# A graph layer on one core: 109 instead of 113 one-hot picked edge sets, 945 instead of 865 gathered chunks, and another order of the opening transfers

## The chip, the cores and the metric

The kernel runs on one core of one Trainium2 chip. The metric is the device time of one execution in microseconds, lower is better. A profile is one more execution under the hardware profiler; it has its own time and its own span, from the first to the last instruction. TensorE is called PE in the profile (PEld: its weight loads), VectorE DVE, ScalarE ACT, GpSimd POOL, SyncE SP; a letter q behind a name is that engine's instruction queue, which issues transfers and waits.

## The reference

There are 12,500 nodes with 128 features and 400,000 edges, sorted by destination, each of one of two types. Every edge carries its source's row through one of two weight matrices, and the messages are summed by destination:

```python
Xs = X[src]
m_data = Xs @ W_data.T + b_data
m_ctrl = Xs @ W_control.T + b_control
msg = jnp.where((edge_types == 0)[:, None], m_data, m_ctrl)
agg = jax.ops.segment_sum(msg, dst, num_segments=X.shape[0])
out = jax.nn.relu(agg + (X @ W_self.T + b_self))
return _layernorm(x + out, axis=-1)
```

## The kernel before

The kernel sums source rows first, by destination and type, and multiplies the sums by the weights afterwards. Each f32 row of x is split into three bf16 parts (high, middle, low) whose sum is the row; the parts stand in SBUF as `x3` and, written out, in DRAM as `rows3` (384 numbers per node).

**Two ways to fetch rows.** The 400,000 edges are 3125 chunks of 128, in 25 groups of 125 chunks. A group is laid out as five times 5 chunks for the first way and 20 for the second.

- *Gathered* chunks (`fetch`, L721; `gathered`, L727): GpSimd issues one indirect DMA that reads the 128 source rows of a chunk from `rows3` into `msg`. VectorE makes a one-hot matrix `psel` (edge by destination and type), once for a window of 5 or 25 chunks. TensorE then does four matmuls: the three parts of `msg` against `psel` (L671) and a column of ones against it, which counts edges (L747). They go to one PSUM bank `sums` for the whole window.
- *Picked* sets (`give_slots`, L518; `picked`, L753): a set is 20 chunks, 2560 edges. VectorE, with some matmuls of TensorE, gives each edge a place in a table of 100 cells by 32 places. The table goes to DRAM (`there`, L624) and comes back to all partitions (`pick`, L626), and VectorE turns it into one-hot columns (L656). TensorE picks the rows out of `x3` with them (`got`, L769), ScalarE casts them to bf16 (`emsg`, L780), and TensorE sums them by destination against a one-hot matrix `esel` (L671, counts in L798). Edges that find their cell full, at most 64, have their rows fetched by an indirect DMA of GpSimd (`last`, L784), the set's *spare rows*. The set's matmuls end with `last`.

In a group with fewer than five picked sets the last gathered window takes the remaining 20 chunks over: it has PL = 25 chunks instead of PB = 5. Before the change every odd group has four sets, every even one five (L175, L181): 113 sets, and 25 x 25 + 12 x 20 = 865 gathered chunks.

**Sums.** When a window or a set is finished, VectorE adds its PSUM bank into the accumulator `acc` of the group (`accumulate`, L702; the line in the profile is L709). A set's add has 352 elements per partition, a window's 160 or 480. There are two PSUM banks `sums` for sets and windows together. When the last window of a group is closed, the group is finished: `pass_on` (L695), then `finish`, which multiplies the sums by the weights (L894), applies the norm and writes out.

**Order.** The program is written as one loop over the sets (L981). Set w carries its own picking and summing, the slot work of sets w+2 and w+3, and its share of the gathered chunks, which are spread evenly over all sets from w = LAG = 2 on (L973). Message gathers are issued AHEAD = 14 chunks before use into HOLD = 18 buffers. A scheduler then orders each engine's instructions, so what stands next to each other in the code need not in the queue. Every engine works its queue in order; SP's transfers wait in order too.

**Opening.** The work from L947 on prepares group 0, splits x, makes the slots of sets 0 and 1, loads the edges of group 1 (`load(1, "e")`, `load(1, "p")`) and writes the bias rows: `bparts` (L395) splits the three biases into bf16 parts on one partition, then copies them into the rows of `bias` with 27 small DMAs (L405, L407). `bias` is first read by the first `finish`. After these come `store_rows` (L259), which writes `x3` to `rows3` in eight DMAs (L261), the first `prep_p`, and the first 14 gathers. All these transfers but x's own loads and the gathers are issued by SP. A gather, of messages as of spare rows, reads `rows3`, so it can run only when all eight stores have landed. The spare rows of a set are fetched at its step t = 2 of six (`spare_rows`, L782).

Of the kernel before, what the change touches and what calls it, by code (L numbers as in the profile page):

```python
# [9 lines left out]
BF = mybir.dt.bfloat16  # L10
# [7 lines left out]
P = 128  # L18
D = 128
# [4 lines left out]
NG = NC // GC  # L24
GN = P * GC * N // E
PB = 5
PL = 25
EC = 20
CQ = EC // 4
NE = 5  # L30
NWIN = 2 * NE
# [11 lines left out]
NQ = 25  # L43
NCELL = 4 * NQ
OVF = 64
# [106 lines left out]
def short_path(ctx, tc, const, ident, eps, wT, brow, bad, x, src, dst, etype, ws, bs, out):  # L152
    nc = tc.nc
    keep = ctx.enter_context(tc.tile_pool(name="keep", bufs=1))
    dram = ctx.enter_context(tc.tile_pool(name="dram", bufs=1, space=DRAM))
# [4 lines left out]
    two = ctx.enter_context(tc.tile_pool(name="two", bufs=2))  # L160
# [4 lines left out]
    def windows(g):  # L165

        c = g * GC
        for i in range(NE):
            yield "p", i, c, PB
            yield "e", i, c + PB, EC  # L170
            c += PB + EC

    def of_p(g, i):

        return PL if g % 2 and i == NE - 1 else PB  # L175

    def edges(a, c, n):
        return a[c * P:(c + n) * P].rearrange("(p c) -> p c", c=n)

    rows_p = (NE - 1) * PB + PL  # L180
    each_e = [(g, i) for g in range(NG) for i in range(NE - g % 2)]  # L181
    raw = {}
    starts = {k: [c for kind, _, c, _ in windows(0) if kind == k] for k in "pe"}
    gap = PB + EC
# [1 line left out]
    def load(g, kind):  # L186
        names = ("src", "dst", "typ")
        if kind == "e":
            raw[kind, g] = [ld.tile([P, NE, EC], I32, name=f"e{name}") for name in names]
            c = g * GC + starts["e"][0]  # L190
            for t, a in zip(raw[kind, g], (src, dst, etype)):
                at = a[c * P:(c + gap * (NE - 1)) * P].rearrange("(i k) -> i k", k=gap * P)[:, :EC * P]
                nc.sync.dma_start(out=t[:, :NE - 1, :], in_=at.rearrange("i (p c) -> p i c", c=EC))
                nc.sync.dma_start(out=t[:, NE - 1, :], in_=edges(a, c + gap * (NE - 1), EC))
        else:
            raw[kind, g] = [ld.tile([rows_p, P], I32, name=f"p{name}") for name in names]
            c = g * GC
            for t, a in zip(raw[kind, g], (src, dst, etype)):
                for i in range(NE):
                    b, n = c + starts["p"][i], PL if i == NE - 1 else PB  # L200
                    nc.sync.dma_start(
                        out=t[i * PB:i * PB + n, :], in_=a[b * P:(b + n) * P].rearrange("(c p) -> c p", p=P)
                    )
# [18 lines left out]
    for kind, i, c, _ in windows(0):  # L222
        if kind == "p":
            n = PL if i == NE - 1 else PB
            nc.sync.dma_start(
                out=near_i[i * PB:i * PB + n, :],
                in_=dst.rearrange("(o g e) -> o g e", o=1, g=NG)[:, :, c * P].to_broadcast([n, NG]),
# [6 lines left out]
    rows3 = dram.tile([N, 3 * D], BF, name="rows3")  # L234
# [44 lines left out]
    bias = keep.tile([P, 2, D], BF, name="bias")  # L279
# [77 lines left out]
    def places_and_weights():  # L357
# [34 lines left out]
            nc.tensor.transpose(wps[:, i * D:(i + 1) * D], wn[:, i, :], ident)  # L392
        nc.scalar.copy(wT, wps[:, :3 * D].rearrange("p (i d) -> p i d", d=D))

    def bparts():  # L395

        part = tmp.tile([1, 3, 3, D], BF, name="part")
        rest = tmp.tile([1, 3, D], FP, name="rest")
        nc.vector.tensor_copy(part[:, 0], brow)
        nc.vector.tensor_tensor(rest, brow, part[:, 0], op=OP.subtract)  # L400
        nc.vector.tensor_copy(part[:, 1], rest)
        nc.vector.tensor_tensor(part[:, 2], rest, part[:, 1], op=OP.subtract)
        for at in [at + k for at in range(0, P, CAP) for k in (0, 3)]:
            for j in range(3):
                nc.sync.dma_start(out=bias[at + j:at + j + 1, :, :], in_=part[:, j, 0:2, :])  # L405
        for j in range(3):
            nc.sync.dma_start(out=bias[6 + j:7 + j, 0, :], in_=part[:, j, 2, :])  # L407


    codes = {}  # L410
# [19 lines left out]
    def prep_p(g):  # L430

        s, d, t = raw.pop(("p", g))
        n = rows_p
        sf = pre.tile([n, P], FP, name="psf")
        rel = pre.tile([n, P], FP, name="prel")

        def first():
            nc.vector.tensor_copy(sf, s)
            nc.vector.tensor_scalar(rel, d, raw["near"][:, g:g + 1], None, op0=OP.subtract)
            codes["n", g] = code_of(rel, t, PW, 0, "p")  # L440

        def then():
            ps = ps1.tile([P, 512], FP, name="fin")
            nc.tensor.transpose(ps[:, :n], sf, ident[:n, :n])
            nc.tensor.transpose(ps[:, 128:128 + n], codes.pop(("n", g)), ident[:n, :n])
            idx = pre.tile([P, n], I32, name="pidx", bufs=3)
            nc.scalar.copy(idx, ps[:, :n])
            codes["p", g] = (idx, twice("pcol2", ps[:, 128:128 + n]))

        return [first, then]  # L450
# [19 lines left out]
    slots = {}  # L470
# [190 lines left out]
    acc, added, parts_in = {}, [], {}  # L661
# [32 lines left out]

    def pass_on(g):  # L695

        assert parts_in[g] == NWIN - g % 2
        if g + 1 < NG:
            begin_acc(g + 1)
            added.append(nc.vector.tensor_add(acc[g + 1][:, :, :lap], acc[g + 1][:, :, :lap], acc[g][:, :, GN:]))  # L700
# [26 lines left out]
    def gathered(g, i):  # L727
# [22 lines left out]

        return evenly([lambda c=c: chunk(c) for c in range(n)])

    def picked(w, tiled, ending, fin_used, before):  # L753

        g, i = each_e[w]
        s = {"sel": {}, "msg": {}}
        per, pair = 4, 2

        def choose(q0, n=8):

            sel = select(sp.tile([P, 9, 2 * EW], BF, name="esel")[:, :n], code_col, slots[w]["code"][:, q0:q0 + n])
            for k in range(n):
                s["sel"][q0 + k] = sel[:, k]

        def pick(ps, q, a0=0):
            for a in range(a0, 4):
                nc.tensor.matmul(  # L769
                    ps[CAP * a:CAP * (a + 1), :], slots[w]["pick"][:, a * NQ + q, :],  # L770
                    x3[:, 4 * q + a - a0].rearrange("p j d -> p (j d)"), start=True, stop=True, skip_group_check=True,
                )

        def rows(q):
            ps = psg.tile([P, pair, 512], FP, name="got")
            msg = two.tile([P, pair, 3 * D], BF, name="emsg", bufs=5)
            for k in range(pair):
                pick(ps[:, k, :3 * D], q + k)
                s["msg"][q + k] = msg[:, k, :]
            nc.scalar.copy(msg, ps[:, :, :3 * D])  # L780

        def spare_rows():  # L782
            msg = s["msg"][NQ - 1] = two.tile([P, 3 * D], BF, name="last")
            nc.gpsimd.indirect_dma_start(  # L784
                out=msg[:OVF, :], out_offset=None, in_=rows3[:, :],
                in_offset=bass.IndirectOffsetOnAxis(ap=slots[w]["idx"], axis=0),
            )

        def last_rows():
            q = NQ - 1  # L790
            ps = psg.tile([P, pair, 512], FP, name="got")[:, 0] if fin_used else ps1.tile([P, 512], FP, name="fin")
            pick(ps[:, :3 * D], q, 2)
            nc.scalar.copy(s["msg"][q][OVF:, :], ps[OVF:, :3 * D])

        def count(q):
            if q == 0:
                s["ps"] = sums()
            nc.tensor.matmul(  # L798
                cells_of(s["ps"], EW, 1)[CAP * (q % 4):CAP * (q % 4 + 1), :], one_col[:, :CAP], s["sel"][q],
                start=(q < 4), stop=(q + 4 >= NQ), skip_group_check=True,  # L800
            )

        def add(q0, q1):
            for q in range(q0, q1):
                add_rows(cells_of(s["ps"], EW, 0), s["msg"].pop(q), s["sel"][q], False, q == NQ - 1)

        def unit(t):

            for q in range(t * per, (t + 1) * per, pair):
                rows(q)  # L810
            if t == 1 and before:
                before()
            if t in (0, 1):
                choose(8 * t)
            if t == 0:
                ending()
            if t == 2:
                spare_rows()
            if t == 3:
                choose(16, 9)  # L820
            if t > 0:
                for q in range((t - 1) * per, t * per if t < turns - 1 else NQ):
                    count(q)
            if t == turns - 1:
                last_rows()
            if t > 0:
                add((t - 1) * per, t * per)
            for u in tiled.get(t, []):
                u()

        def end():

            add((turns - 1) * per, NQ)
            for u in tiled.get(turns, []):
                u()
            accumulate(g, 2 * i + 1, s["ps"], EW, EW)

        turns = (NQ - 1) // per
        return evenly([lambda t=t: unit(t) for t in range(turns)]), end


# [105 lines left out]
    split_units.pop(0)()  # L947
    prep_e(0)
    merged([(0.97, places_and_weights)], evenly(all_slots(0) + all_slots(1)), evenly(split_units))
    load(1, "e")  # L950
    load(1, "p")
    bparts()
    early.close()
    pro.close()
# [4 lines left out]
    for u in begin_slots(2):  # L959
        u()  # L960
    store_rows()
    for u in prep_p(0):
        u()
    for _ in range(AHEAD):
# [6 lines left out]
    for p in range(NG * NE):  # L971
        for _, u in gathered(*divmod(p, NE)):
            at = LAG + (n + 0.5) * (pairs - LAG) / total  # L973
# [206 lines left out]
```

## Time and profile before

| | us |
|---|---|
| median of 3 runs | 2086.24 |
| lowest and highest | 2075.97, 2093.50 |
| the profiled execution | 2095.26 |
| its span, first to last instruction | 2093.6 |

The profile's page has the busy time of each engine and its share of the span, the chain of work that ended last, and groups of instructions by line. A group's row reads: line, engine, operation, what it writes and reads, how often; then its busy time (the union of its instructions, in us), the mean duration of one in ns, and the idle time of the engine just before them with what ended most of it. A matmul's end is modelled and consecutive matmuls overlap, so the mean is longer than what one adds to a dense stream. A timeline's row reads: start, duration, engine, line, operation, what it writes and reads; in brackets the idle time before it and what ended it. Rows of the DMA queues give when a transfer was issued, not when it landed. The table of stretches gives, for each stretch, its length, the busy time of each engine with the number of its instructions, the granted clock of TensorE, the busy share of the DMA engines and their rate. TensorE's mean granted clock over the execution is 0.978. By the page's chain, 57% of the span is TensorE's, 28% VectorE's, 5% ScalarE's.

### The profile page before, as it was taken

To read this page: it belongs to the slowest core of one execution; us is meant where nothing else is said; L and a number is where in the kernel's file an instruction comes from. 1 tells how busy PE (TensorE), PEld (TensorE's weight loads), DVE (VectorE), ACT (ScalarE), POOL (GpSimd) and SP (SyncE) were. 2 spreads that over 40 slices of the span, in tenths; PEclk is the share of its full clock that TensorE was granted. 3 is DMA by queue.
4 is the path that set the end of the run, shared out by engine and by line. 5 is a ranking of instruction groups with operands and counts; after the bars stand their busy time and mean duration, and the time that the engine had idled before them with its cause. 6 is when DMAs were issued, how large, how long until landed. Compare 5 with 4: busy or idle time off the path is not lost.

```text
span 2093.6 us, 75473 instructions
## 1 busy us (share of the span) xinstructions
PE 1836.4 (88%) x30869; PEld 1376.5 (66%) x30869; DVE 1720.3 (82%) x4707; ACT 1304.5 (62%) x2464; POOL 1305.9 (62%) x996
## 2 busy tenths in 40 slices
PE   0669889999999998999999999999999999999996
PEld 0446667666766676666666666766776676766675
DVE  7958889888888888888888878878888888878873
ACT  4535666666666665666666666656666666656665
POOL 0167667667667566667666556575667667766760
PEclk9989999999999999999999999999999999999998
DMA  7643443443443443433433434434434434434321
GB/s 187 193 123 115 122 136 101 137 135 100 133 135 99 135 133 95 137 111 117 135 108 108 127 99 136 131 100 134 132 102 132 131 111 131 120 105 130 124 96 32
DMA packets 187343, 254.92 MB, mean 122 GB/s; under 512 B 86202, under 2 KB 153804, under 8 KB 183916
## 3 DMA queue, kind: packets, MB, share of 16 engines
q1 hardware_dynamic: 129226, 152.97, 22.7%
q0 software_dynamic: 45136, 90.65, 15.5%
q10 hardware_dynamic: 12626, 6.40, 1.2%
q8 instruction: 243, 3.98, 0.8%
q14 instruction: 112, 0.92, 0.1%
HBM read 231.87 MB, written 18.03 MB: 119 GB/s over the span
## 4 chain that ended last, share of the span: by engine, by line
PE 57%; DVE 28%; issue 5%; ACT 5%; DMA 2%; SPq 1%; POOL 1%; DVEq 0%; another core or an unknown queue 0%; ACTq 0%; POOLq 0%
PE sums L671 25%; PE got L769 19%; ACT emsg L780 4%; DVE esel L476 3%; PE rk L614 3%; DVE pick L656 3%; DVE prod L564 3%; DVE rv L602 2%; PE sums L798 2%; PE fin L894 2%; DVE found L573 2%; DVE prod L542 2%; PE rk L502 2%; DVE ahead L560 2%; PE rk L550 1%
## 5 line engine op out<-in xcount | busy, mean ns | idle before, releaser
L721 POOL DMA_INDIRECT msg<-rows,pidx x865 | 1167.3, 1350 | 697.9 <-PE sums L671 236.2
L780 ACT CAST emsg<-got 128x768 bf16<-128x768 f32 x1356 | 1036.1, 803 | 522.6 <-PE got L769 387.6
L671 PE MATMUL sums<-esel,emsg 128*128 128x176 bf16 x8136 | 761.9, 242 | 14.3 <-issue 13.4
L769 PE MATMUL got<-x,pick 128*32 128x384 bf16 x10896 | 663.5, 334 | 77.5 <-ACT emsg L780 43.8
L671 PEld LDWEIGHTS <-emsg 128*128 128x128 bf16 x8136 | 603.0, 99 | 174.6 <-issue 157.6
L769 PEld LDWEIGHTS <-pick 128*32 128x32 bf16 x11074 | 258.7, 95 | 232.6 <-issue 131.2
L476 DVE TENSOR_TENSOR esel<-code_col,code 128x1408 bf16<-128x1408 bf16 x339 | 308.6, 910 | 31.7 <-PE sums L671 14.1
L709 DVE TENSOR_TENSOR acc<-acc,sums 128x352 f32 (+2 forms) x238 | 102.0, 428 | 175.3 <-PE sums L671 85.8
L671 PE MATMUL sums<-psel,msg 128*128 128x48 bf16 x2595 | 187.3, 185 | 17.5 <-issue 7.2
L798 PE MATMUL sums<-esel,one_col 128*32 128x176 bf16 x2825 | 181.7, 244 | 7.0 <-issue 6.3
L784 POOL DMA_INDIRECT last<-rows,idx x113 | 134.4, 1189 | 56.4 <-issue 16.5
L671 PEld LDWEIGHTS <-msg 128*128 128x128 bf16 x2595 | 150.7, 98 | 26.0 <-issue 23.6
L614 PE MATMUL rk<-rv,O 128*128 128x64 bf16 x2260 | 90.8, 195 | 70.9 <-DVE rv L602 64.8
L656 DVE TENSOR_SCALAR pick<-pick,lane_f 128x1600 bf16<-128x1600 bf16 x226 | 143.2, 639 | 8.5 <-issue 5.0
L614 PEld LDWEIGHTS <-O 128*128 128x128 bf16 x2260 | 83.1, 100 | 99.2 <-issue 98.3
L747 PE MATMUL sums<-psel,one_col 128*128 128x48 bf16 x865 | 145.9, 183 | 0.5 <-issue 0.5
L476 DVE TENSOR_TENSOR O<-cell_col,blk 128x2000 bf16<-128x2000 bf16 x113 | 134.6, 1191 | 12.2 <-PE fin L769 4.7
L564 DVE TENSOR_TENSOR prod<-O,ahead 128x2000 bf16<-128x2000 bf16 x113 | 134.4, 1189 | 0.0
L560 DVE TENSOR_REDUCE ahead<-rk 128x100 bf16<-128x500 f32 x113 | 76.2, 674 | 53.5 <-PE got L769 21.0
L798 PEld LDWEIGHTS <-one_col 128*32 128x32 bf16 x2825 | 86.6, 96 | 47.5 <-issue 17.7
L747 PEld LDWEIGHTS <-one_col 128*128 128x128 bf16 x865 | 82.9, 96 | 1.0 <-issue 0.9
L573 DVE TENSOR_REDUCE found<-half 128x20 f32<-128x520 bf16 x113 | 77.1, 683 | 0.0
(173 smaller groups left out, 2030.2 us busy)
## 6 DMA issues: line engine op xcount, KB each, us to landing
pick<-there SPq DMA_DIRECT2D x113, 800.0 KB
acc<-acc_start SPq DMA_DIRECT2D x23, 1280.0 KB
msg<-rows,pidx POOLq DMA_INDIRECT x865
rows<-x SPq DMA_DIRECT2D x6, 1344.0 KB
xs<-in_x_dram SPq DMA_DIRECT2D x99, 62.5 KB
out_dram<-h SPq DMA_DIRECT2D x99, 62.5 KB
xt<-in_x_dram ACTq DMA_DIRECT2D x6, 896.0 KB
there<-cell SPq DMA_DIRECT2D x113, 6.2 KB
```

Of the source, the lines that this page charges most:

```text
L476: nc.vector.tensor_tensor(sel.rearrange("p n (w t) -> p n w t", t=2), col[:rows].rearrange("p (o w t) -> p o w t", o=1, t=2).to_broadcast( ...
L564: nc.vector.tensor_tensor(prod, s["O"], ahead.rearrange("p (o j) -> p o j", o=1).to_broadcast([P, EC, NCELL]), op=OP.mult)
L573: nc.vector.tensor_reduce(found, half[:, :, :26], AX.X, OP.add)
L614: nc.tensor.matmul(s["rk"][:m, :2 * CAP], s["held"][:, c * NCELL:c * NCELL + m], s["rv"][:, c].rearrange("p v r -> p (v r)"), start=(c == ...
L656: nc.vector.tensor_scalar(t, t, lane_f, None, op0=OP.is_equal)
L671: nc.tensor.matmul(out, msg[:, j * D:(j + 1) * D], sel, start=(start and j == 0), stop=stop, skip_group_check=True)
L721: nc.gpsimd.indirect_dma_start(out=msg[:, k, :], out_offset=None, in_=rows3[:, :], in_offset=bass.IndirectOffsetOnAxis(ap=codes["p", g][0] ...
L747: nc.tensor.matmul(cnt, one_col, sel, start=False, stop=(c == n - 1), skip_group_check=True)
L769: nc.tensor.matmul(ps[CAP * a:CAP * (a + 1), :], slots[w]["pick"][:, a * NQ + q, :], x3[:, 4 * q + a - a0].rearrange("p j d -> p (j d)"), ...
L780: nc.scalar.copy(msg, ps[:, :, :3 * D])
L784: nc.gpsimd.indirect_dma_start(out=msg[:OVF, :], out_offset=None, in_=rows3[:, :], in_offset=bass.IndirectOffsetOnAxis(ap=slots[w]["idx"], ...
L798: nc.tensor.matmul(cells_of(s["ps"], EW, 1)[CAP * (q % 4):CAP * (q % 4 + 1), :], one_col[:, :CAP], s["sel"][q], start=(q < 4), stop=(q + 4 ...
```

## The change

It has two parts. First, of three groups one now has five picked sets and two have four: groups 0, 3, 6, ..., 24 have five. In the others the last gathered window has 25 chunks. Second, the opening transfers are arranged anew: the biases' parts go to DRAM in one DMA (`b_parts`) and come back with nine (three rows at a time) in place of the 27 copies; the loads of group 1 are written behind the stores of `rows3`; the spare rows of set 0 are fetched ahead of the first 14 message gathers instead of in the middle of set 0.

```diff
+    def sets(g):
+        return NE if g % 3 == 0 else NE - 1
+
     def of_p(g, i):
-        return PL if g % 2 and i == NE - 1 else PB
+        return PL if sets(g) < NE and i == NE - 1 else PB
...
-    each_e = [(g, i) for g in range(NG) for i in range(NE - g % 2)]
+    each_e = [(g, i) for g in range(NG) for i in range(sets(g))]
...
+    b_parts = dram.tile([3, 3, D], BF, name="b_parts")
+
     def bparts():
...
         nc.vector.tensor_tensor(part[:, 2], rest, part[:, 1], op=OP.subtract)
+        nc.sync.dma_start(
+            out=b_parts.rearrange("j i d -> (j i d)").rearrange("(o e) -> o e", o=1),
+            in_=part.rearrange("o j i d -> o (j i d)"),
+        )
+
+    def bias_rows():
         for at in [at + k for at in range(0, P, CAP) for k in (0, 3)]:
-            for j in range(3):
-                nc.sync.dma_start(out=bias[at + j:at + j + 1, :, :], in_=part[:, j, 0:2, :])
-        for j in range(3):
-            nc.sync.dma_start(out=bias[6 + j:7 + j, 0, :], in_=part[:, j, 2, :])
+            nc.sync.dma_start(out=bias[at:at + 3, :, :], in_=b_parts[:, 0:2, :])
+        nc.sync.dma_start(out=bias[6:9, 0, :], in_=b_parts[:, 2, :])
...
-        assert parts_in[g] == NWIN - g % 2
+        assert parts_in[g] == NE + sets(g)
...
+    def spare_rows(w):
+        msg = slots[w]["last"] = two.tile([P, 3 * D], BF, name="last")
+        nc.gpsimd.indirect_dma_start(
+            out=msg[:OVF, :], out_offset=None, in_=rows3[:, :],
+            in_offset=bass.IndirectOffsetOnAxis(ap=slots[w]["idx"], axis=0),
+        )
...
             if t == 2:
-                spare_rows()
+                if w > 0:
+                    spare_rows(w)
+                s["msg"][NQ - 1] = slots[w]["last"]
...
     merged([(0.97, places_and_weights)], evenly(all_slots(0) + all_slots(1)), evenly(split_units))
-    load(1, "e")
-    load(1, "p")
     bparts()
...
     store_rows()
+    spare_rows(0)
+    bias_rows()
+    load(1, "e")
+    load(1, "p")
     for u in prep_p(0):
```

More of the change, by code (lines that the diff above doesn't have):

```diff
@@ L780, in rows @@
             nc.scalar.copy(msg, ps[:, :, :3 * D])
[L782 to L787, printed above, removed]
         def last_rows():
```

## Prediction

> **What bounds the kernel now.** I read the page's busy shares first, then busy time by stretch, then the timelines of the stretch that a stretch-table made look odd, then waits and groups for prices.
>
> ```profile
> span 2093.6 us, 75473 instructions
> PE 1836.4 (88%) x30869; PEld 1376.5 (66%) x30869; DVE 1720.3 (82%) x4707; ACT 1304.5 (62%) x2464; POOL 1305.9 (62%) x996
> ```
> ```profile
> core 0: us, PE busy (x) PEld busy (x) DVE busy (x) ACT busy (x) POOL busy (x), PEclk, DMA share, GB/s
> 60.00:95.14 35.14, 27.17 (x375) 17.34 (x375) 32.63 (x92) 21.93 (x44) 0.01 (x1) 1.00 0.56 170
> 95.14:126.20 31.06, 12.37 (x166) 8.41 (x168) 11.00 (x35) 8.16 (x17) 22.27 (x21) 0.71 0.54 169
> 126.20:2045.30 1919.10, 1760.38 (x29794) 1322.77 (x29787) 1614.62 (x4415) 1225.57 (x2336) 1277.47 (x956) 0.99 0.39 120
> ```
> Third row of the table: TensorE is busy for 92% of the long middle, VectorE 84%, GpSimd 67%, DMA 39%. The middle is TensorE's. Second row: from 95 to 126 us TensorE works 12.4 of 31.1 us. That is a hole in the opening.
>
> The middle is cut into sets by VectorE's add of a picked set into `acc` (128x352), once per set:
>
> ```profile
> 126.22 0.52 DVE L709 TENSOR_TENSOR acc<-acc,sums 128x352 f32 x1
> ...
> 2045.25 0.52 DVE L709 TENSOR_TENSOR acc<-acc,sums 128x352 f32 x1 [0.57 <-PE sums L671]
> ```
> These are sets 1 and 110 (counting from 0), so one set takes (2045.25 - 126.22) / 109 = 17.61 us. From the times of all such adds, the 24 sets in which a group is finished (L894) run 2.7 us longer than the rest; that part belongs to groups, not to sets.
>
> The hole, in the timelines of SP's queue, GpSimd and TensorE:
>
> ```profile
> 62.13 7.42 SPq L405 DMA_DIRECT2D bias<-part  x9
> ...
> 74.00 6.82 SPq L405 DMA_DIRECT2D bias<-part  x11
> 80.86 1.85 SPq L407 DMA_DIRECT2D bias<-part  x3
> 82.76 6.44 SPq L261 DMA_DIRECT2D rows<-x  x3
> ```
> ```profile
> 95.14 2.95 POOL L721 DMA_INDIRECT msg<-rows,pidx  x1 [90.33 <-DMA edst<-in_dst_dram]
> ...
> 115.72 0.91 POOL L784 DMA_INDIRECT last<-rows,idx  x1 [0.30 <-issue]
> 116.93 0.91 POOL L784 DMA_INDIRECT last<-rows,idx  x1 [0.30 <-issue]
> ```
> ```profile
> 118.34 0.62 PE L671 MATMUL sums<-esel,last 128*128 128x176 bf16 x3 [10.40 <-DMA last<-rows,idx]
> ```
> 27 small bias copies stand on SP in front of the last three pieces of `rows3`. No gather can run before these land, so GpSimd starts at 95.14. Fourteen message gathers then stand in front of the spare rows (`last`) of sets 0 and 1, and TensorE, done with the rest of both sets at 107.95, waits until 118.34.
>
> **The change: four sets fewer, 80 chunks more.** Groups 0, 3, ..., 24 (9) have five sets, 16 have four: 45 + 64 = 109 sets. Chunks: 25 x 25 + 16 x 20 = 945. They are spread over all sets but the first two, as now: 865 / 111 = 7.79 per set become 945 / 107 = 8.83. What a chunk costs TensorE is the open term:
>
> ```profile
> 1007.70 0.23 PE L671 MATMUL sums<-psel,msg 128*128 128x48 bf16 x3
> 1007.78 0.18 PE L747 MATMUL sums<-psel,one_col 128*128 128x48 bf16 x1
> 1007.89 0.51 PE L769 MATMUL got<-x,pick 128*32 128x384 bf16 x8
> ```
> ```profile
> L671 PE MATMUL sums<-psel,msg 128*128 128x48 bf16 x2595 | 187.3, 185 | 17.5 <-issue 7.2 <-DVE acc L709 7.2 <-DMA msg<-rows,pidx 1.4
> L747 PE MATMUL sums<-psel,one_col 128*128 128x48 bf16 x865 | 145.9, 183 | 0.5 <-issue 0.5
> ```
> From below: in a dense stretch (timeline) a chunk's four matmuls start at 1007.70 and the next work at 1007.89: 0.19 us. From above: the groups' busy time, (187.3 + 145.9) / 865 = 0.385 us, which counts the pipeline's drain where the next matmul already runs. I take 0.25, nearer to the direct reading. Then of a set's 17.61 us, 7.79 x 0.25 = 1.95 are chunks, 24 x 2.7 / 109 = 0.59 groups, and 15.07 the set itself. After: 15.07 + 8.83 x 0.25 + 24 x 2.7 / 105 = 17.89 us for each of the 105 sets between the same two marks: 1878.5 against 1919.0, a gain of 40. With 0.19 it is 46 (set alone 15.54, new period 17.83), with 0.385 it is 25 (14.02 and 18.04).
>
> A sentence beside it: the Trainium skill ("Perfetto Trace Analysis", Identifying the Most-Contended Engine) calls matmul busy time a bad measure, since matmuls are pipelined, and counts LDWEIGHTS busy instead. This profile's weight loads of a chunk, 150.7 + 82.9 us over 865, give 0.27 us and a gain of 38 by that rule; the trace agrees in so far as 0.27 lies between the two readings above.
>
> Off TensorE: VectorE loses four sets' work (1614.62 us over 109 sets, groups' work included: at most 14.8 us each) and gains 80 / 5 = 16 five-chunk selections' worth of work at 0.326 us: no new bound. ScalarE loses 48 copies of 0.80 us. GpSimd is the one engine that gains work:
>
> ```profile
> L721 POOL DMA_INDIRECT msg<-rows,pidx x865 | 1167.3, 1350 | 697.9 <-PE sums L671 236.2 <-PE got L769 178.5 <-DMA edst<-in_dst_dram 90.3
> ```
> A gather takes 1.35 us and 0.30 to the next: 1.65. With 1.5 for the set's `last` (1.19 + 0.30), a set takes 7.79 x 1.65 + 1.5 = 14.4 of 17.61 us now and 16.1 of 17.89 after, 90%. It now waits for TensorE to free buffers (236.2 and 178.5 us), and TensorE waited 1.4 us in all for a gathered message. So I cost it at nothing; the cover is some 1.8 us per set.
>
> **The change: the opening.** 27 bias copies (18.5 us of SP) become one write of `b_parts` and nine reads. In the built order of the changed program the stores of `rows3` stand among the loads of group 1, and the last one right behind set 1's `there` copy and `b_parts`; VectorE's order up to there is unchanged. Its last piece of x is done at 65.75, that `there` is ready at 68.2, so the store goes at about 69.5 instead of the three stores' 82.76 to 89.20. From the end of that issue to the first gather were 5.9 us: the gathers start at about 75.5, 20 us sooner. Set 0's `last` is first and lands by 78 (from its issue to landing 2.2 us). Behind it stand 18 gathers, 14 ahead and four of set 2, at 1.255 us (start to start here): set 1's `last` is issued at 75.5 + 1.25 + 22.6 = 99.3 and lands by 102, before TensorE needs it at 107.95. The 10.4 us wait is gone, and with it the slow train behind (add of set 0 at 124.04, 4.0 us more of TensorE idle for its bank). Set 1's add comes at about 108 instead of 126.2: a gain of 18. What is late next is TensorE's own stream of two sets. Bounds: up to 25 if the gaps of 0.4 us between its matmuls from 102 to 108 go too; 0 if another transfer takes the place.
>
> The wait that it adds: the bias reads wait on SP for `b_parts` to land. Queued behind: nine reads (0.6 us each by the rows above), the loads of group 1's edge types, group 2's edges and then set 2's `there`, which now goes at 89.30. `b_parts` goes at about 69; the worst small copy of this stretch, `there` at 53.48, landed after 7.3 us behind stores. 69 + 7.3 + 5.4 + 11 issues at 0.3 to 0.5 = 87: in time by 2 us, and each us beyond costs set 2 one. ScalarE's zeroing of `acc`, which shares memory with `part`, stands earlier in its queue and also waits for that copy, with set 0's casts behind: 0 to 3 us, inside the bounds.
>
> **Rivals.** (a) The opening gives nothing, since another transfer (the earlier stores compete with the fetches of x) delays the first `pick`. For it: DMA is 56% busy there. Against: the new order takes 17 issues off the queue. Gain 40 alone: 2086 - 40 = 2046.
> (b) The middle gives nothing: idle of TensorE (159 us of the 1919, 1.46 per set) grows because ScalarE's casts and the picks' matmuls alternate with more chunk matmuls between. It needs 0.39 us more per set, 41 in all. For it: 43.8 us of `got` waiting for casts. Gain 18 alone: 2068.
> (c) Slower: GpSimd already sets the pace. Its chunk then costs what it takes all in, (17.61 - 1.5) / 7.79 = 2.07 us, so a set takes 8.83 x 2.07 + 1.5 = 19.8 us, and 105 of them 2079: +160 - 18, or 2228. The change loses from 18.45 us per set on (1919 + 18 over 105), that is 1.92 us per gather. For it: by the trace, the 707 gathers and spare-row fetches beside which VectorE was busy for at least nine tenths of their first 0.9 us averaged 1.45 us, against 0.94 for the 85 beside which it was idle. Against: even 1.45 for all would be 8.83 x 1.75 + 1.5 = 17.0 us per set, and GpSimd waits for TensorE, not the reverse. The Trainium skill ("SBUF — State Buffer", A bandwidth-pool intuition that's wrong) says that a GpSimd-issued DMA of 620 ns takes about 3100 ns beside a VectorE copy, since VectorE locks out the writing of descriptors. At that length on every gather a set would be 8.83 x 3.4 + 1.5 = 31.5 us and the run over 3400, with no chance beside rows that stand at 17.61 with 7.79 chunks: the trace (mean 1.35, longest 4.26) bears out the lock, not that length.
> That the counts are not as said is no rival: the built order has 109 and 945.
>
> **How the numbers follow.** Likeliest: 40 + 18 = 58 less. The profiled execution took 2095.26 us (span 2093.6), 9.0 over the median of 2086.24; 2095.3 - 58 = 2037 on its own scale, 2028 on the median's. Its own range is 46 + 25 to 25 + 0 less: 2015 to 2061. Chances: forecast 0.68, (a) 0.17, (b) 0.09, (c) 0.06. A measurement here can tell about 1%, 21 us: faster below 2065 (forecast and (a), 0.85), within it (b), slower (c). For 8 in 10 the range takes in the forecast's ends, (a), and some 4 us of the runs' scatter: 2010 to 2064.
>
> **What would show it.** In the changed profile: the first gather near 75 and no wait for `last` near 10 us; set 1's add near 108; 105 periods of 17.9 us; GpSimd idle still ended by TensorE; TensorE's wait for messages still a few us. Wrong if the period exceeds 18.2, if GpSimd's idle is ended by nothing but issue, or if set 0 starts later than 69.

## The result, and the profile after

The changed kernel took 2190.87 us (median of 4 runs, 2187.47 to 2196.01), the kernel before beside it 2082.16 us (4 runs, 2075.97 to 2093.50): 1.049 times as long, 95% interval 1.0456 to 1.0525 (the two medians alone give 1.052; ratios here are always the recorded ones, differences in us are those of medians). Forecast were 2028 us and faster. The profiled execution took 2196.01 us with a span of 2193.9.

Page and table of stretches of the changed kernel, columns as before:

```profile
span 2193.9 us, 74107 instructions
...
PE 1859.7 (85%) x30253; PEld 1373.7 (63%) x30253; DVE 1673.0 (76%) x4583; ACT 1264.0 (58%) x2392; POOL 1397.7 (64%) x1072
```
```profile
core 0: us, PE busy (x) PEld busy (x) DVE busy (x) ACT busy (x) POOL busy (x), PEclk, DMA share, GB/s
60.00:77.10 17.10, 8.77 (x96) 5.24 (x96) 17.10 (x44) 7.60 (x15) 0.00 (x0) 1.00 0.77 268
77.10:107.80 30.70, 15.62 (x207) 9.86 (x206) 10.20 (x31) 11.99 (x22) 21.83 (x19) 0.78 0.43 127
122.71:2145.05 2022.34, 1780.63 (x29159) 1316.66 (x29156) 1566.94 (x4286) 1184.48 (x2263) 1366.21 (x1031) 0.96 0.38 116
```
In the long middle TensorE's share fell from 92% to 88%, VectorE's from 84% to 77%, ScalarE's from 64% to 59%. GpSimd's rose only from 67% to 68%. There is more time, and no engine fills it.

The sets' adds (timeline of VectorE; sets 0, 1 and 106):

```profile
107.25 0.52 DVE L719 TENSOR_TENSOR acc<-acc,sums 128x352 f32 x1 [20.08 <-issue]
...
122.19 0.52 DVE L719 TENSOR_TENSOR acc<-acc,sums 128x352 f32 x1 [0.38 <-PE sums L681]
...
2144.53 0.52 DVE L719 TENSOR_TENSOR acc<-acc,sums 128x352 f32 x1 [1.60 <-PE sums L681]
```
One set takes (2144.53 - 122.19) / 105 = 19.26 us, where 17.89 was forecast and 17.61 stood before. Over 105 sets the miss is 144 us, nearly all of the distance between forecast and result (163). Of the 1.65 us that a set takes longer than before, TensorE's busy rows hold 0.81 (16.15 to 16.96) and its idle time 0.84 (1.46 to 2.30).

TensorE's granted clock fell too, from 0.99 to 0.96 in the middle. By the clock's records it stood at half for 57 us of the middle before and for 143 us after. In these stretches TensorE began 9.9 and 8.1 instructions per us, in the rest 15.7 and 14.9. If the clock alone made that difference, it cost 21 us before and 65 after, so at most some 44 of the 173 us by which 105 periods grew. That is an estimate from these figures; what lowered the clock is not shown.

GpSimd's group on the page, its timeline in the opening, then TensorE's and ScalarE's in the same stretch:

```profile
L731 POOL DMA_INDIRECT msg<-rows,pidx x945 | 1260.6, 1334 | 636.4 <-PE sums L681 209.1
```
```profile
77.11 2.60 POOL L765 DMA_INDIRECT last<-rows,idx  x1 [72.30 <-DVE prod L574]
80.02 0.98 POOL L731 DMA_INDIRECT msg<-rows,pidx  x1 [0.30 <-issue]
...
103.47 0.95 POOL L731 DMA_INDIRECT msg<-rows,pidx  x1 [0.30 <-issue]
108.37 2.38 POOL L765 DMA_INDIRECT last<-rows,idx  x1 [3.95 <-DVE worst L426]
```
```profile
97.41 0.82 PE L786 MATMUL got<-x,pick 128*32 128x384 bf16 x6 [2.11 <-issue]
98.62 0.48 PE L786 MATMUL got<-x,pick 128*32 128x384 bf16 x1 [0.39 <-issue]
100.05 0.48 PE L786 MATMUL got<-x,pick 128*32 128x384 bf16 x1 [0.95 <-issue]
106.60 1.04 PE L786 MATMUL got<-x,pick 128*32 128x384 bf16 x8 [6.06 <-issue]
```
```profile
96.56 0.80 ACT L797 CAST emsg<-got 128x768 bf16<-128x768 f32 x1 [1.99 <-PE rk L512]
105.75 0.80 ACT L797 CAST emsg<-got 128x768 bf16<-128x768 f32 x1 [8.39 <-remote]
```
The gathers do start 18 us sooner (77.11 for 95.14). But while GpSimd issues them without a pause, TensorE does 16 matmuls in 10 us. The cast at 105.75 reads the eight matmuls whose last one ended at 100.05 + 0.48 = 100.53: it starts 5.2 us after its input was done by the profile, and the record of TensorE's completion signal, which ScalarE waits for, stands at 105.67. The eight matmuls at 106.60 then start 0.05 us after this cast's end (105.75 + 0.80). So the opening's gain is gone at once: set 0's add comes 17 us sooner than before, set 1's four, and set 3's is later (161.44 for 159.06).

TensorE's waits (what it waited for: us in all, times, longest):

```profile
PE got L786 <- issue: 75.8, 148, 6.1
...
PE got L786 <- ACT emsg L797: 48.2, 85, 3.5
PE sums L681 <- issue: 31.9, 89, 1.1
```
"Issue" means that the profile shows nothing that it waited for. That has two main causes here. Of the 132.7 us of such waits of TensorE in the whole run, 96.6 stand before matmuls that wait for no signal at all, as the 0.39 and 0.95 above. 27.7 end within 0.12 us of the end of an instruction of ScalarE or VectorE whose signal has no record, as the 6.06: there TensorE did wait for the cast.

**Two kinds of sessions.** The experiments ran in five sessions, each on one chip, each beside its own runs of the kernel before. These runs agree within a session to about 1%, but not between sessions: 2094, 2112 and 2089 us in three, as in the first measurement, and 1948 and 1951 in two. I call them slow and quick sessions. The expectations below, written before that was complete, say slow and quick chip; one chip number, 0, appears on both sides, so whether it is the chip or its surroundings is not known. Ratios are against the kernel before of the same session.

### The profile page after: what moved, and what is told of

Read it like the earlier page. It is cut to its first block, busy times and chain, and to the rows that moved or that the text cites. A ratio compares the mean times of both kernels' runs of the same rounds, so it can differ in the third digit from the quotient of the medians.

```text
span 2193.9 us, 74107 instructions
## 1 busy us (share of the span) xinstructions
PE 1859.7 (85%) x30253; PEld 1373.7 (63%) x30253; DVE 1673.0 (76%) x4583; ACT 1264.0 (58%) x2392; POOL 1397.7 (64%) x1072
## 4 chain that ended last, share of the span: by engine, by line
PE 55%; DVE 28%; issue 7%; ACT 4%; DMA 2%; another core or an unknown queue 2%; DVEq 0%; SPq 0%; POOL 0%; ACTq 0%; POOLq 0%
PE sums L681 24%; PE got L786 19%; DVE esel L486 3%; ACT emsg L797 3%; PE rk L624 3%; DVE prod L574 3%; DVE pick L666 3%; PE sums L808 2%; DVE rv L612 2%; DVE found L583 2%; DVE ahead L570 2%; DVE prod L552 2%; PE rk L512 1%; PE rk L560 1%
## 5 line engine op out<-in xcount | busy, mean ns | idle before, releaser
L731 POOL DMA_INDIRECT msg<-rows,pidx x945 | 1260.6, 1334 | 636.4 <-PE sums L681 209.1
L797 ACT CAST emsg<-got 128x768 bf16<-128x768 f32 x1308 | 1000.8, 803 | 587.2 <-PE got L786 371.5
L786 PE MATMUL got<-x,pick 128*32 128x384 bf16 x10512 | 684.7, 338 | 129.8 <-issue 75.8
L681 PE MATMUL sums<-esel,emsg 128*128 128x176 bf16 x7848 | 751.2, 245 | 21.7 <-issue 21.1
L681 PEld LDWEIGHTS <-emsg 128*128 128x128 bf16 x7848 | 592.2, 100 | 182.1 <-issue 167.4
L486 DVE TENSOR_TENSOR esel<-code_col,code 128x1408 bf16<-128x1408 bf16 x327 | 298.1, 912 | 40.8 <-PE sums L681 22.0
L681 PE MATMUL sums<-psel,msg 128*128 128x48 bf16 x2835 | 198.7, 186 | 20.2 <-issue 10.4
L681 PEld LDWEIGHTS <-msg 128*128 128x128 bf16 x2835 | 160.8, 98 | 35.7 <-issue 30.9
L757 PE MATMUL sums<-psel,one_col 128*128 128x48 bf16 x945 | 155.8, 184 | 1.6 <-issue 1.6
L757 PEld LDWEIGHTS <-one_col 128*128 128x128 bf16 x945 | 91.3, 97 | 4.1 <-issue 4.1
```

What stands on the lines that cost most here:

```text
L486: nc.vector.tensor_tensor(sel.rearrange("p n (w t) -> p n w t", t=2), col[:rows].rearrange("p (o w t) -> p o w t", o=1, t=2).to_broadcast( ...
L681: nc.tensor.matmul(out, msg[:, j * D:(j + 1) * D], sel, start=(start and j == 0), stop=stop, skip_group_check=True)
L731: nc.gpsimd.indirect_dma_start(out=msg[:, k, :], out_offset=None, in_=rows3[:, :], in_offset=bass.IndirectOffsetOnAxis(ap=codes["p", g][0] ...
L757: nc.tensor.matmul(cnt, one_col, sel, start=False, stop=(c == n - 1), skip_group_check=True)
L786: nc.tensor.matmul(ps[CAP * a:CAP * (a + 1), :], slots[w]["pick"][:, a * NQ + q, :], x3[:, 4 * q + a - a0].rearrange("p j d -> p (j d)"), ...
```

## The experiments

Gathers are message gathers, without the sets' `last`. In the traces the extra or left-out ones number 79. In the row marked (m) the extra gathers take buffers of the 18 that the message gathers use; the other extra gathers have a buffer of their own.

| kernel | gathers / sets | slow session | quick session |
|---|---|---|---|
| whole change | 945 / 109 | 1.049 [1.0456, 1.0525] | 0.983 [0.9775, 0.9885] |
| new opening alone | 865 / 113 | 0.9996 [0.9961, 1.0031] | |
| new sets alone | 945 / 109 | 1.0425 [1.0374, 1.0477] | |
| whole change, 79 gathers left out | 866 / 109 | 1.0073 [1.0039, 1.0108] | |
| before, 79 full gathers more (m) | 944 / 113 | 1.0718 [1.065, 1.0787] | |
| before, 79 full gathers more | 865 + 79 / 113 | | 1.0091 [1.006, 1.0123] |
| ... of 16 rows | 865 + 79 / 113 | 1.0517 [1.045, 1.0585] | 1.0097 [1.0056, 1.0137] |
| ... of 64-byte rows | 865 + 79 / 113 | 1.0522 [1.0456, 1.0588] | 1.0096 [1.0066, 1.0126]; 1.009 [1.0059, 1.0122] |
| before, 79 iotas on GpSimd more | 865 / 113 | 1.0027 [0.9997, 1.0058] | 1.0004 [0.9978, 1.003] |
| before, 79 reads by SP more | 865 / 113 | 0.9977 [0.9946, 1.0008] | 1.0055 [1.0033, 1.0078] |
| new opening, 117 sets | 785 / 117 | 0.994 [0.9916, 0.9964] | 1.0237 [1.0185, 1.029] |
| whole change, shorter lead | 945 / 109 | 1.0312 [1.0235, 1.0389] | |

### One part of the change at a time

The new opening with the sets of before, and the new sets with the opening of before:

```diff
     def sets(g):
-        return NE if g % 3 == 0 else NE - 1
+        return NE - g % 2
```


> The new opening alone; 113 sets and 865 gathered chunks as before. Theory G (the gathers themselves slow the rest of the chip: about 2 us for each one added, wherever it stands) and theory S (the new layout of windows and sets is worse, gathers or not): the opening is worth what the adds of sets 0 to 3 show, about nothing by set 3, so within 10 us of the kernel before, near 2080. Theory O (the other order of instructions that the new opening brings slows the long middle): most of the 109 us of the whole change, above 2150. The prediction on record would have 18 less than before, 2064.

> The 109 sets and 945 chunks alone, with the opening of before. G and S: 2185 to 2200, as the whole change. O: about 40 less than before, 2040, as the prediction's term for the middle has it.

Both in a slow session (before 2093.84): 2093.13 and 2178.11 us. The new opening with its new order of instructions costs nothing and is worth nothing (0.9996); the loss comes with sets and gathers (1.0425 of the 1.049, in another session; 2178 lies 7 us below the range of G and S). So the theory of the order (O) fell, and the other two (G, S) stood.

### Gathers without their matmuls, matmuls without their gathers

From the changed kernel, every twelfth gather is left out (first diff). To the kernel before, every eleventh is added a second time (second diff):

```diff
         if to_fetch:
...
+            if len(to_fetch) % 12 == 6:
+                fetched.append(fetched[-1] if fetched else last_msg[0])
+                return
             msg = mp.tile([P, SB, 3 * D], BF, name="msg")
+            last_msg[:] = [msg]
```
```diff
             fetched.append(msg)
+            if len(to_fetch) % 11 == 6:
+                nc.gpsimd.indirect_dma_start(
+                    out=mp.tile([P, SB, 3 * D], BF, name="msg")[:, 0, :], out_offset=None, in_=rows3[:, :],
+                    in_offset=bass.IndirectOffsetOnAxis(ap=codes["p", g][0][:, at:at + 1], axis=0),
+                )
```


> The changed kernel, with 78 of its 945 gathers left out, evenly spread: the chunk's four matmuls run as before but read the rows of the chunk before it. So 867 gathers, about as many as before the change, and four sets fewer; the sums of those chunks are other ones. G: before less four sets (4 x 15.07 us), plus 80 chunks' matmuls (0.25 us each), about 2040. S and O: gathers are no matter, 2180 to 2195.

> The kernel before, with 78 gathers more (every 11th chunk is gathered a second time, into a buffer that nobody reads): 943 gathers, no other work added. G: 78 x 1.4 to 2.1 us more, 2190 to 2245. S and O: GpSimd has 1.8 us of slack in each set, so within 10 us of before, 2080 to 2092.

Same slow session: 2109.50 and 2235.99 us. 79 gathers that nobody reads cost 142 us, 1.80 each, more than the whole change. That is theory G's number, without any new layout. The other run is a miss for both: 2110 lies 70 above G's 2040 and 70 below S's 2180. Against the new sets alone in the same session (2178.11) the 79 gathers left out bring back 69 us, 0.87 each. That is most of the loss against the kernel before (84 us), but at half the price of an added gather, and with as many gathers as before and four sets fewer the kernel is no faster than before. Why the four sets' work that goes away is not won here stays open: the layout (S) is refuted as the whole cause, not as a part of it in such a session.

### What of a gather is it?

Four small additions to the kernel before, in the places of the extra gathers, into a buffer of their own (the memory of `first_i`, dead by then). Shown are the gather of 16 rows, the iota and the read by SP; the short gather has 128 rows of 32 numbers:

```diff
+                nc.gpsimd.indirect_dma_start(
+                    out=spare_buf[:16, :192].bitcast(BF), out_offset=None, in_=rows3[:, :],
+                    in_offset=bass.IndirectOffsetOnAxis(ap=at[:16], axis=0),
+                )
...
+                nc.gpsimd.iota(first_all, pattern=[[NG * NE, 2], [NE, NG], [1, NE]], base=0, channel_multiplier=0)
...
+                nc.sync.dma_start(out=spare_buf[:, :192].bitcast(BF), in_=rows3[:P, :])
```


> The kernel before with 78 extra gathers, each of 16 rows instead of 128, into a buffer of their own that nobody reads. 78 full ones cost 142 us, 1.82 each. Theory Q (GpSimd's time is what costs; an extra instruction on its queue delays the rest): about as much per us of GpSimd, so 80 to 140 more if a small gather takes as long there, near 2200. Theory R (the rows, one transfer descriptor each, are what costs): an eighth, 18 more. Theory B (the bytes moved): an eighth, 18 more.

> The kernel before with 78 extra gathers of 128 rows of 64 bytes instead of 768. Q: 110 to 140 more. R: all of the 142 more, near 2235. B: a twelfth, 12 more.

> The kernel before with 78 extra iota instructions on GpSimd (128x250 int32, about 1 us each) in the places of the extra gathers; no transfer. Q: 80 to 110 more. R and B: nothing, within 10 us of before.

> The kernel before with 78 extra plain reads of 128 rows (768 bytes each, 98 KB in all) of the same DRAM tensor, issued by SP, in the places of the extra gathers. Q: nothing. R and B: if what counts is rows or bytes on the transfer engines, whoever issues them, the whole 142 more; if only gathers weigh, nothing.

It was a quick session (before 1948.22): 20, 21, 4 and 12 us more. No theory had expected that small gathers cost so little, because none had expected the session. In its traces ScalarE's casts of picked rows start on time: 4 of 1214 start more than 0.3 us after all they need (kernel with the iotas, 200 to 1850 us), in the first profile of the kernel before 189 of 1122. To find out whether the cost of a gather is tied to the session, four kernels ran next: the changed kernel itself again, a version of it with 117 sets,

```diff
     def sets(g):
-        return NE if g % 3 == 0 else NE - 1
+        return NE - 1 if g % 3 == 1 else NE
```
and with the extra gathers to the separate buffer in full (128 rows of 768 bytes) and in short rows again.

> The changed kernel once more, since the kernel before took 2094 us on one chip (call it slow) and 1948 on another (quick), and on the quick one small extra gathers cost 0.26 us each. Theory G (a gather costs 1.8 us wherever it runs): 1.04 to 1.05 times before on either chip. Theory H (only on the slow chip does a gather hold up TensorE; on the quick one TensorE's completions follow its matmuls in 0.19 us, gathers running or not): on a slow chip 1.045, on a quick one faster than before, 0.97 to 0.99, near what the prediction on record works out.

> The new opening, and of three groups two with five picked sets and one with four (groups 1, 4, ..., 22): 117 sets, 785 gathered chunks, 80 gathers fewer than before and four sets more. G: four sets at 15 us less 80 gathers at 1.82 is 86 us less than before on either chip. H: 86 less on a slow chip, 30 to 40 more on a quick one. The prediction's prices: 40 more on either.

> The kernel before with 78 extra full gathers (128 rows of 768 bytes) into the buffer of their own, in the same places. G: 142 more on either chip. H: 142 more on a slow chip, 20 to 40 on a quick one.

> The 78 extra gathers of 128 rows of 64 bytes again. On a quick chip 20 more, as measured. On a slow one, theory R (rows, one transfer descriptor each, hold TensorE up): 142 more; theory B (the bytes moved): 12 more.

Quick again (before 1950.59): 1921.73, 1995.81, 1964.00 and 1968.11 us. The changed kernel is faster here, by 1.7%, and 79 full gathers cost 13 us, 0.17 each, not 142. The extra gathers here have a buffer of their own, those of the 142 had not; but the small ones, with their own buffer in both kinds of session, differ between them too (below). G falls as a price of the gather as such. H is right in both signs; its sizes were off (20 to 40 us for the full gathers, 30 to 40 for the 117 sets, which lost 45). Of the changed kernel in the quick session, a row of the table of stretches around a train of gathers, the train in GpSimd's timeline, and TensorE's waits:

```profile
757.80:765.40 7.60, 7.60 (x146) 5.66 (x135) 6.98 (x22) 5.89 (x12) 5.73 (x7) 1.00 0.59 190
```
```profile
757.84 0.96 POOL L731 DMA_INDIRECT msg<-rows,pidx  x1 [0.30 <-PE rk L624]
759.10 0.95 POOL L731 DMA_INDIRECT msg<-rows,pidx  x1 [0.30 <-issue]
...
764.10 0.95 POOL L731 DMA_INDIRECT msg<-rows,pidx  x1 [0.30 <-issue]
```
```profile
PE rk L624 <- DVE rv L612: 88.9, 75, 19.1
PE sums L681 <- DMA last<-rows,idx: 39.6, 9, 14.6
...
PE got L786 <- ACT emsg L797: 10.9, 30, 0.9
```
And the same row for two trains in the slow session, the one in the opening and one in the middle:

```profile
87.20:104.40 17.20, 5.37 (x62) 2.72 (x60) 0.00 (x0) 1.62 (x4) 13.22 (x14) 0.71 0.43 131
2084.40:2091.60 7.20, 4.45 (x71) 2.90 (x69) 1.00 (x9) 1.95 (x4) 5.63 (x6) 0.98 0.57 196
```
GpSimd issues one gather per 1.25 us in all three. TensorE is busy all of 7.60 us in the quick session and begins 19 matmuls per us (146 / 7.60); in the slow one it begins 3.6 in the opening (62 / 17.20), where VectorE begins none, and 9.9 in the middle (71 / 7.20). Of the waits on "issue", 75.8 and 31.9 us above, the quick session has none.

How late an instruction starts can also be counted without those labels. A cast of picked rows needs the end of its eight matmuls, the end of ScalarE's instruction before it, and the end of the matmuls that read its buffer last (five casts earlier). Between 200 and 1850 us of the changed kernel, in the slow session, 196 of 1027 casts start more than 0.3 us after the last of these, 234 us in all; in the quick one 4 of 1181, 1.5 us in all. It goes with the number of gathers, `last` included, that start in the 6 us around. TensorE's rate is counted in stretches of 6 us:

| gathers in 6 us | 1 | 2 | 3 | 4 | 5 |
|---|---|---|---|---|---|
| slow: casts start late by, mean us | -0.01 | 0.02 | 0.19 | 0.46 | 0.89 |
| quick | -0.04 | -0.01 | -0.01 | 0.00 | -0.01 |
| slow: TensorE's instructions begun per us | 16.3 | 15.5 | 14.6 | 13.3 | 8.9 |
| quick | 16.3 | 16.7 | 16.7 | 16.8 | 15.5 |

The slow column for five gathers rests on 5 casts and 22 stretches that overlap. (Below zero, a cast starts before the modelled end of its last matmul.) The records of TensorE's completion signals say the same: between 60 and 1850 us, 965 of 2757 stand more than 0.3 us after the matmul's modelled end and at no other matmul's end in the slow session, none of 3172 in the quick one. Whether the matmul itself ends later than its row or the signal travels longer can't be told apart. For VectorE and ScalarE such a count says nothing: the slow session's trace lacks records (VectorE has 2990 for 3792 signals, in the quick session 3726), and every record of theirs that seems late stands within 60 ns of the end of a later instruction of the same engine. Of the 224 casts whose record seems late, 72 had a reader on TensorE that had begun before it. Why records are missing, and whether taking the trace has a share in the delays, is not known.

The Trainium skill ("Perfetto Trace Analysis", Per-engine timelines) says that a semaphore's propagation lies behind the window that the profiler reports for a VectorE or ScalarE instruction. The trace agrees: in the quick session the signal's record stands 0.01 us (median) behind the row's end for both engines.

### The same again in slow sessions

Two more sessions, both slow (before 2112.50 and 2088.79). The kernels are those above, with one new: the changed kernel with a shorter lead.

```diff
-HOLD = 18
-AHEAD = 14
+HOLD = 6
+AHEAD = 3
```


> The changed kernel with 6 message buffers instead of 18 and 3 gathers ahead of use instead of 14, so that GpSimd can not issue long trains of gathers back to back. The chips so far: before takes 2094 us on one (slow) and 1948 to 1951 on two (quick); the changed kernel is 1.045 times before on a slow one and 0.983 on a quick one. In the traces of the slow chip TensorE starts 4 instructions per us where five gathers stand in 6 us, and 15 to 19 where one to three do; on the quick one 15 to 17 either way. Theory T (on a slow chip the trains hold TensorE up, not the single gather): on a slow chip shorter trains give most of the loss back, 1.00 to 1.02 times before. Theory G1 (each gather costs 1.8 us there, in a train or not): 1.04 to 1.05. On a quick chip, either: 0.98 to 0.995, a little lost to messages that come later.

> The 78 extra gathers of 16 rows again, for a slow chip: there 78 full ones cost 142 us. Theory Q (GpSimd's part of a gather counts): 80 to 140 more. R (the rows, one descriptor each): 18 more, plus the 20 that it costs on a quick chip. B (bytes): the same 18 to 38 more. On a quick chip 20 more, as measured.

> The 78 extra gathers of 128 rows of 64 bytes, for a slow chip. Q and R: 110 to 142 more. B: 12 to 30 more. On a quick chip 20 more, as measured.

> The 78 extra plain reads issued by SP, for a slow chip. Q, and R if only gathers' descriptors count: 0 to 12 more. B, and R if any descriptor counts: 142 more. On a quick chip 12 more, as measured.

Measured: 2177.59, 2223.48, 2221.49 and 2106.85 us. Extra gathers of an eighth of the rows or a twelfth of the bytes cost 111 and 109 us, 1.4 each, against 1.80 for full ones; no run has full ones in a buffer of their own in a slow session, so how much of the 0.4 is size stays open. 79 reads of the same bytes by SP cost nothing (interval 0.9946 to 1.0008). So neither bytes (B) nor rows (R) make up most of the price; theory Q's range holds the number. GpSimd's groups with short rows in the slow session:

```profile
L723 POOL DMA_INDIRECT msg<-rows,pidx x865 | 1156.5, 1337 | 655.4 <-PE sums L673 191.5 <-PE got L777 183.1 <-issue 111.1
...
L730 POOL DMA_INDIRECT first_all<-rows,pidx x79 | 98.4, 1246 | 80.3 <-DMA first_all<-rows,pidx 43.1 <-ACT pcol L429 17.9 <-issue 16.3
```
A gather of 64-byte rows takes GpSimd 1.25 us, a full one 1.34: it is held nearly as long. (These extra gathers also waited 43.1 us in all for their buffer, which may be part of the 109.)

The shorter lead (1.0312) lies between the two theories. It also made no clean test: of the gathers from 200 us on, 111 stood in trains of four or more (started under 1.35 us apart) in the changed kernel and 84 with the shorter lead. And most of what it wins is won in the opening, where 3 gathers instead of 14 stand ahead: set 1's add comes at 106.46 us, 122.19 in the changed kernel's first profile, while a set of the middle takes 19.24 us, 19.26 there (two sessions, 1.5% apart by the kernel before). Whether the train or each gather is to blame in the middle stays open.

> The 78 extra iota instructions of 1 us on GpSimd, for a slow chip, where 78 extra gathers of 16 rows cost 111 us, of 128 short rows 109, and 78 plain reads by SP nothing. Theory Q1 (any instruction of GpSimd holds the others up there): 80 to 110 more. Theory Q2 (only what GpSimd does to issue a transfer): 0 to 10 more. On a quick chip 3 more, as measured.

> The new opening with 117 sets and 785 gathers again, for a slow chip; on a quick one it took 1.024 times before, 45 us more. Theory H (on a slow chip a gather costs 1.4 to 1.8 us, with its chunk's matmuls or without): four sets at 15 us less 80 gathers, so 52 to 86 less than before there, 0.96 to 0.975: the signs of both directions of the change swap between the chips. If the slow chip loses by any departure from the old pattern of sets: 1.02 or more there too.

Measured: 2093.27 and 2076.02 us. An iota on GpSimd costs nothing:

```profile
L730 POOL IOTA first_all<- 128x250 int32 x79 | 69.1, 875 | 21.0 <-DVE from_f L371 15.7
```
0.875 us of GpSimd each, no transfer, and 1.0027 (interval with 1 in it). So Q1 falls and Q2 stands: what holds the others up belongs to a transfer that GpSimd issues, and most of it to a part that does not grow with rows or bytes. Whether that is GpSimd's own work or something in the transfer's way is not separated. The 117 sets swap their sign as expected (0.994 in a slow session, 1.024 in a quick one), but they gain 13 us, not 52 to 86. Set periods say the same: in slow sessions 16.82 us with 785 gathers, 17.61 with 865, 19.26 with 945, so the second 80 gathers cost twice as much as the first (0.79 and 1.65 us per set). The price rises with the density.

No kernel here is the best in both kinds of session: the changed one is best in quick ones, 117 sets with the new opening in slow ones.

## Why the prediction was wrong, step by step

- **The failed step: "So I cost it at nothing; the cover is some 1.8 us per set."** GpSimd's added gathers were taken to be hidden because GpSimd had idle time and TensorE hardly waited for messages (1.4 us in all). In slow sessions, the first measurement among them, a gather holds up the other engines, however idle GpSimd is otherwise: 1.80 us per full one added with no other work. 80 of them are 144 us, the size of the middle's miss, but that the two agree is in part luck: a gather left out brings back 0.87 us, so the price is not constant. The gathers account for most of the loss against the kernel before (69 of 84 us); that the gain of 40 did not come on top is not explained. Up to some 44 us may have passed through the lower clock. In quick sessions the step nearly holds: 0.17 to 0.26 us each.
- **What the trace of before already showed.** TensorE beside GpSimd's train, in the timeline of the kernel before:

```profile
105.47 0.31 PE L671 MATMUL sums<-esel,emsg 128*128 128x176 bf16 x2 [0.38 <-issue]
106.22 0.31 PE L671 MATMUL sums<-esel,emsg 128*128 128x176 bf16 x2 [0.44 <-issue]
106.94 0.39 PE L671 MATMUL sums<-esel,emsg 128*128 128x176 bf16 x3 [0.40 <-issue]
107.71 0.24 PE L671 MATMUL sums<-esel,emsg 128*128 128x176 bf16 x1 [0.38 <-issue]
```
  The prediction named these gaps of 0.4 us and took them for a chance of 7 us more; what lies beside them is a gather each 1.25 us. In that trace 189 of 1122 casts start more than 0.3 us late (200 to 1850 us), 195 us in all. With 17% of them late, "nothing" had no row to stand on.
- **The price of a chunk, 0.25 us (0.19 to 0.385).** In quick sessions the period rose from 16.31 us (the kernel with the iotas, 1.0004 times before) to 16.73: with 0.02 for groups that leaves 0.40 for 1.04 chunks, 0.38 each, the upper end. From 117 sets (16.13, 6.83 chunks per set) to 113 it is (16.31 - 16.13 - 0.02) / 0.96 = 0.17, just below the lower end. Both ends were seen; the middle's gain there is 109 x 16.31 - 105 x 16.73 = 21 us, not 40.
- **The opening, a gain of 18 (0 to 25).** The gathers start at 77.11, forecast 75.5; SP's part was right. The new opening alone is worth nothing (0.9996 in a slow session; it was not run alone in a quick one). In the slow session TensorE stands beside the train. In the quick one it runs, set 0's add comes at 89.04, and the wait for spare rows moves to set 1 (14.6 us): its `last` is issued at 113.75, forecast 99.3, because the 18 gathers before it took 33.8 us beside a busy VectorE (2.68 to 5.44 us for some) and not 22.6. The forecast had taken their 1.255 us from a train beside which VectorE was idle. Set 1's add comes at 119.76 there, forecast 108.
- **The rivals.** (a), the opening gives nothing, is right that it gave nothing, by other mechanisms. (b), TensorE's idle time grows by the casts, is right that it grows (1.46 to 2.30 us per set, more than the 0.39 it asks for) and wrong about why: in the middle the picks' waits on casts went from 43.4 to 46.7 us, TensorE's waits on "issue" from 54.5 to 118.8. (c), 0.06, comes nearest in time: 2228, with 2.07 us per chunk all in; 19.8 us per set against 19.26. Its place was wrong: GpSimd does not set the pace by being full (68% of the middle, and most of its idle time is ended by TensorE). That its price came near is luck in good part: it divides a whole set's time by its chunks, while the period rose by 1.65 us for 1.04 chunks, 1.59 each, and by 0.82 each from 785 to 865 gathers.
- **"Wrong if the period exceeds 18.2"** said it: 19.26.

What stays open: what makes a session slow or quick, by which path GpSimd's gathers delay TensorE's completions and its next instruction, what lowers the clock, why four sets fewer win nothing in a slow session, and the price of a lone gather against one in a train.

## What to carry to other kernels

An engine's idle time is cover for its own work only: before more gathers are put on GpSimd, look in the timeline at what the other engines do beside a dense train of them, and at whether a waiter starts when its producer's row ends. A doubled gather that nobody reads prices it, and so does leaving one out; the two prices need not agree (1.80 and 0.87 us here). And run a change of this kind in more than one session: its sign differed between two (1.049 and 0.983), while each session by itself looked certain.

## What the hardware showed that was not expected

- In slow sessions the gathers that GpSimd issues hold up TensorE's completions (a cast that started 5.2 us after its matmuls' rows had ended) and its next matmuls, and the transfer's size matters little (1.80 us for 98 KB in the message buffers; in a buffer of their own 1.40 for an eighth of the rows, 1.38 for a twelfth of the bytes). 0.9 us of other work on GpSimd and SP's reads of the same rows cost nothing.
- The kernel before takes 2082 to 2112 us in one kind of session and 1948 to 1951 in the other, with TensorE's mean granted clock at 0.978 in the first profile and 0.988 in the profile of the kernel with the iotas in a quick one; in slow sessions 0.981 to 0.988 occur too, so the clock does not explain it.
- The Trainium skill ("SBUF — State Buffer", A bandwidth-pool intuition that's wrong) has a DMA issued by GpSimd wait for VectorE, 620 ns alone and about 3100 beside a copy. The trace agrees in kind (0.94 us beside an idle VectorE, 1.55 beside one busy throughout its first 0.9 us in the changed kernel's first profile, single ones to 5.44 in the quick session). The reverse, which decided this case, is the delay of TensorE, and of those that wait for it, by GpSimd's gathers.
